# Where one gate product stands, and in which order the first pair's loads, stores and inner sums are issued

## Chip, core and metric

The kernel runs on one core of a Trainium2 chip, in one launch. The metric is device time in microseconds (us), from start to end of the program. The core has engines that run side by side, each with its own queue, strictly in order: TensorE (PE in the profile, PEld for its weight loads), VectorE (DVE), ScalarE (ACT), GpSimd (POOL) and SyncE (SP, which issues most DMA transfers). They wait for each other through semaphores. Matrix products land in PSUM banks, everything else lies in SBUF.

## What is computed

Inputs are x (32 x 128 x 512, float32), a condition vector per batch row, a mask, and the weights of two layers. Here B = 32, S = 128, D = 512, the inner width of the second layer is 1024, everything is float32.

```python
m = mask[:, :, None]
emb = silu(t) @ ada_w + ada_b
shift, scale, gate_msa = split(emb, 3, axis=1)
norm = layernorm(x) * (1.0 + scale[:, None]) + shift[:, None]
norm = where(m, norm, 0.0)
fwd = gelu(norm @ ssm_w1 + ssm_b1) @ ssm_w2 + ssm_b2
bwd = flip(gelu(flip(norm) @ bwd_w1 + bwd_b1) @ bwd_w2 + bwd_b2)
x = x + gate_msa[:, None] * where(m, fwd + bwd, 0.0)

ff_ada = silu(t) @ ffada_w + ffada_b
shift_mlp, scale_mlp, gate_mlp = split(ff_ada, 3, axis=1)
ff_norm = layernorm(x) * (1.0 + scale_mlp[:, None]) + shift_mlp[:, None]
h = gelu_tanh(ff_norm @ ff_w1 + ff_b1)
out = x + gate_mlp[:, None] * (h @ ff_w2 + ff_b2)
```

The two flips cancel, because the network works on each token alone. The first layer touches masked tokens only.

## The kernel before

**First layer ("opening").** The masked tokens get numbers, "slots". Four tiles of 128 slots are gathered from x (L254, issued by POOL). In the opening and up to the end of the pairs the program order is the order on every engine: `tc.manual_schedule` (L385) takes PE, DVE, ACT, POOL and SP as they are written.

The condition's product with ada_w has three column blocks: shift, scale and gate. `ada_a` holds the weights; its shift and scale columns come in four loads (L128), its gate columns in a fifth (L132, through L146). `modulation_matmuls` (L279) forms `pm_ss`, the first two blocks; `modulation_rows` (L289) adds the bias on DVE and writes `mod1`. `slot_part` (L299, `part_s`) spreads rows of `mod1` over the slots with a one-hot matrix; there are four of these, scale and shift for slot tiles 0 and 1. Then comes the gate block in another way: four products `pm_g` (L541), one for each quarter of the depth, side by side in strips of 32 partitions; ACT copies them to `gate_parts` (L544); a product with `strips` (L594, `pm_gate`) adds the four. DVE normalises the slot tiles (L182, L183: `xn_s`), PE transposes them (L190, `ptr_s`), ACT copies the transposes (L191), and `hidden_of_tile` (L574, `ph_s`) starts the hidden layer.

`count_more` (L641) takes eight small DVE steps on a product `pt` (L645). Its results serve a loop after the pairs for masked tokens beyond the slots.

**Second layer ("pairs").** All tokens pass in four pairs; a pair is two sides of four batch rows, 1024 tokens. Both products of the layer are formed by a fast scheme of seven instead of eight block products (P1 to P7), with sums before and after. The first product uses it twice, one in the other: seven outer blocks, here called streams, in the order 1, 2, 5, 6, 3, 7, 4, each of seven inner products. One inner product is four matmuls on PE (L988). "P3 of 2" below is inner product P3 of stream 2.

- `weight_sums(j)` (L634) forms four outer sums of the first weight on DVE. `store_weight_sums` (L638, L639) writes them to `t_rows` in DRAM by SP; their homes are borrowed: number 1 in the spare x tiles, 2 in t_2, 4 in `tw_4`. `load_weights(j)` (L934, tile `tw`) reads one back.
- `TokenBlocks.one` (L857) forms the outer sums of the tokens on DVE; its fourth writes into the memory of `tw_4`.
- `token_sums(j, n)` forms inner sums of the tokens on DVE, for j = 1 (L917, `sx`), 2 (L921, `xn_sy`), 3 (L924) and 4 (L927), each in four parts n. Both operands lie in SBUF.
- ACT copies P5 of each stream to `p5` (L1002) and other products on (L1046), or applies the GELU (L950). DVE adds after P6 (L1013), P7 (L1018) and P4 (L1023), and `seed` (L1032) fills the bank of the next product. POOL adds `with_p5` (L1039), `after` (L1068) and late sums (L1072), again with both operands in SBUF.
- A stream's P3 and P7 wait for L1013 of the same stream, P2 for `seed`, P4 for L1018. L1013 of streams 6 and 3 waits for POOL's sums.
- `window(new, old)` interleaves P5, P1, P2, P6 of the new stream with P3, P7, P4 of the old one and runs `fills`, steps put behind a place (window, position) by `put`.
- `take_first_half` (L747): eight gathers by POOL, which overwrite the masked tokens of the next pair's x with rows from the first layer (`x1_rows`). They stand in POOL's queue between `with_p5` of stream 2 and that of stream 6.
- `load_side` (L351) loads x of a coming side; `fw2_of.combine` (L342) and L1314 form differences of the second weight `fw2`, loaded at L705.

The part of the first pair that stands before its first window is written out by hand (L1291 to L1314); the first layer's last tile is stored just before it (`with_x`, L1274).

Of the kernel before, what the change touches and what calls it, by code (L numbers as in the profile page):

```python
# [9 lines left out]
F32 = mybir.dt.float32  # L10
# [4 lines left out]
ALU = mybir.AluOpType  # L15
# [7 lines left out]
def kernel(  # L23
# [49 lines left out]
    nc = tc.nc  # L73
    B, S, D = x.shape
    P = 128
# [3 lines left out]
    KC = D // P  # L79
# [113 lines left out]
    def hidden(xT, n, w, bcol, func, name, pool, parts=range(HC), after=None):  # L193

        h = []
        for f in parts:
            ph = ps_h.tile([P, 512], F32, tag="h", name=f"ph_{name}_{f}")
            for k in range(KC):
                nc.tensor.matmul(  # L199
                    ph[:, :n], w[:, k, ts(f, P)], xT[:, k, :], start=(k == 0), stop=(k == KC - 1)  # L200
                )
            t = pool.tile([P, n], F32, tag="h", name=f"h_{name}_{f}", bufs=HC)
            nc.scalar.activation(t, ph[:, :n], func, bias=biasT[:, bcol + f : bcol + f + 1])
            h.append(t)
            for g in (after or {}).get(f, ()):
                g()
        return h
# [79 lines left out]
    def modulation_rows(pm, mod, modb, lo, hi):  # L287
        rows = slice(lo * B, hi * B)
        nc.vector.tensor_tensor(mod[rows], pm[rows], modb[rows], ALU.add)  # L289
# [14 lines left out]
    def slot_part(at, j, pool, tag):  # L304
        return of_slots(pick, at, mod1, j, pool, tag, f"part{j}_s{at}")
# [228 lines left out]
    token_i = find_slots(1, (ps_h, "h"))  # L534
    modulation_matmuls(pm, ada_a, 0, 2, range(KC - 1, KC))
    modulation_rows(pm, mod1, modb_a, 0, 2)
    rows = [(slot_part(c, 1, ps_o, "o"), slot_part(c, 0, *((ps_o, "o"), (ps_h, "h"))[c])) for c in range(2)]
    gate_parts = tp.tile([P, D], F32, tag="t", name="gate_parts")
    pm = ps_t.tile([P, 512], F32, tag="tr", name="pm_g")
    for k in range(KC):  # L540
        nc.tensor.matmul(  # L541
            pm[ts(k, B), :], sT[:, k, :], ada_a[:, k, ts(2, D)], start=True, stop=True
        )
    nc.scalar.copy(gate_parts, pm)  # L544
    xT_s = ssm.tile([P, KC, NH], F32, tag="xT", name="xT_s0", bufs=2)
    xT_t = ssm.tile([P, KC, NH], F32, tag="xT", name="xT_s1", bufs=2)
    xn = group_of_tiles("s")
# [3 lines left out]
        modulated(xc[0], *rows[0], "s0", xn[:, 0], (mv[:, 0, 0:1], rstd)),  # L551
        modulated(xc[1], *rows[1], "s1", xn[:, 1]),
    ]
    fw1 = fwp.tile([P, KC, FF], F32, name="fw1")
    fw2 = fwp.tile([P, HC, D], F32, name="fw2")
    t_1 = fwp.tile([P, 3, KC // 2, FF // 2], F32, name="t_1")
# [33 lines left out]
    hidden_of_tile(0, 0)  # L590
    hidden_of_tile(1, 0)
    transposed_slots(xn_s[1], xT_s[:, :, ts(1, P)], "s1")
    pm = ps_o.tile([P, 512], F32, tag="o", name="pm_gate")
    nc.tensor.matmul(pm[ts(2, B), :], strips, gate_parts, start=True, stop=True)  # L594
    modulation_rows(pm, mod1, modb_a, 2, 3)
    hidden_of_tile(2, 0)


# [37 lines left out]
    def store_weight_sums(*which, queue=nc.sync):  # L636
        for j in which:
            queue.dma_start(t_rows[j - 1, :, 4:], t_sum[j][1][:, :3])  # L638
            queue.dma_start(t_rows[j - 1, :, :4], t_sum[j][0])  # L639

    def count_more():  # L641

        pt = ps_t.tile([P, 512], F32, tag="tr", name="pt")
        for j in range(2):
            nc.tensor.matmul(pt[:, j : j + 1], every[:, j], count, start=True, stop=True)  # L645
# [12 lines left out]
        nc.vector.tensor_copy(more_i, more_f)  # L658
        nc.vector.tensor_scalar(more_i, more_i, 7, None, ALU.logical_shift_right)
        col_l = const.tile([P, 1], F32, name="col_l")  # L660
        nc.vector.tensor_scalar(col_l, slot_col[:, 0:1], start_at, None, ALU.add)
        return total, start_at, more_i, col_l


    total, start_at, more_i, col_l = count_more()
    for n, t in enumerate(raw):
        own_statistics(t, 2, f"x_{n}")
    h1 = []
# [19 lines left out]
    nc.vector.tensor_tensor(b2, b2, b2b, ALU.add)  # L688
    b2_row = dram.tile([1, D], F32, name="b2_row")
    with_gated_bias(0, gs[0])  # L690
    h1 += hidden(xT_s, NH, w1, 0, AF.Gelu, "s0", ssm, range(3, HC - 1))
    gate_and_next_tile(1)
    Weights(fw1, KC // 2, FF // 2, t_1).combine(0, 1, 2, 3)
# [8 lines left out]
    finish_slots(1, h1, gs[1])  # L702
    nc.sync.dma_start(b2_row, b2[0:1, :])
    broadcast_rows(fb2, ff_b2, nc.sync)
    nc.sync.dma_start(fw2, ff_w2.rearrange("(k p) f -> p k f", p=P))  # L705

    for c in range(2):
        transposed_slots(xn_late[c], xT_t[:, :, ts(c, P)], f"s{2 + c}")
# [535 lines left out]
    def turn_rows(b):  # L1244
# [6 lines left out]
    after[7] += [  # L1251
        normalised_of_side_1,
        lambda: weight_sums(4),
        lambda: store_weight_sums(1, 2, 4),
        lambda: x_of.update({1: [load_side(1, 0, spare), None]}),
        turn(0),
    ]
# [30 lines left out]
    first_half.close()  # L1288
    hp = straight.enter_context(tc.tile_pool(name="hp", bufs=1))
    gp = straight.enter_context(tc.tile_pool(name="gp", bufs=1))  # L1290
    x_of[1][1] = load_side(1, 1)  # L1291
    now = FirstProduct(0, of_x[0].cut(), of_w)
    for j in (1, 2):
        now.load_weights(j)
    for n in range(4):
        now.token_sums(1, n)
    now.apart(1)
    now.do(1, "P1")
    now.seed(1)
# [1 line left out]
    now.do(1, "P5", "P2", "P6")  # L1301
    now.do(2, "P5")
    now.seed(2)
    now.do(1, "P7")
    now.with_p5(2, "22")
    for n in range(4):
        now.token_sums(2, n)
    now.do(1, "P3")
    now.with_p5(2, "12")
    take_first_half(1, x_of[1])  # L1310
    now.do(2, "P2", "P6")
    now.do(1, "P4")
    fw2_of.combine(0, 1)
    nc.vector.tensor_tensor(fb2_step, fb2[:, D // 2 :], fb2[:, : D // 2], ALU.subtract)  # L1314
    for p in range(NP):
        more_pairs = p + 1 < NP
        xs = x_of[p]
# [2 lines left out]
        def put(w, n, f, *args):  # L1320
            fills.setdefault(w, {}).setdefault(n, []).append(lambda: f(*args))

        if p:
            for n, at in enumerate(((1, 3), (1, 4), (1, 6))):
                put(*at, now.token_sums, 2, 1 + n)
        for n, at in enumerate(((1, 6), (2, 1), (2, 3), (2, 3)) if p else ((2, 3), (2, 3), (2, 4), (2, 4))):
            put(*at, now.token_sums, 3, n)
        for n, at in enumerate(((2, 4), (2, 4), (2, 6), (2, 6)) if p else ((2, 6), (2, 6), (3, 1), (3, 1))):
            put(*at, now.token_sums, 4, n)
        put(3, 6, now.load_weights, 3)  # L1330
        put(4, 6, now.load_weights, 4)
        second = SecondProduct(p, now.h, xs)
        put(6, 0, now.late_gelu, "11")
        put(6, 1, second.seed, 0)
        put(6, 3, second.first_block, 0, 0, 2)
# [227 lines left out]
```

## Time and profile before

| what | us |
|---|---|
| timed runs, median of 4 | 465.69 (464.8 to 466.64) |
| profiled execution, its time | 463.53 |
| its span, first to last instruction | 461.8 |
| PE busy, 0 to 10 | 6.05 |
| PE busy, 10 to 20 | 8.10 |
| PE busy, 90 to 100 | 7.94 |
| PE busy, 100 to 110 | 9.39 |
| PE busy, 110 to 120 | 9.34 |
| PE busy, 130 to 380 | 249.98 |

Times in the trace count from the start of the span. A group line gives start, busy time, engine, source line, operation, output <- inputs, count; in brackets stands the idle time of the engine before it and what ended it. A line of waits says who waited for whom, us in total, how often, and the longest.

On all other engines there is slack: DVE is busy for 334.9 us, POOL for 156.7, ACT for 176.5. In 100 to 110 DVE is busy for 9.96 us and in 110 to 120 POOL for 9.51.

### The profile page before, as it was taken

Reading aid. Unit: us, or ns where it says so; the run is one execution under the profiler, and the core shown is the slowest. Engines: PE = TensorE matmul, PEld = TensorE weight load, DVE = VectorE, ACT = ScalarE, POOL = GpSimd, SP = SyncE. Lnnn points to the kernel's source line nnn. Section 1 sums busy time; section 2 is a strip of 40 time slices with the busy share of each in tenths; the row PEclk is TensorE's granted clock in tenths of the full one; section 3 lists DMA queues with packets and bytes.
Section 4 is the critical chain, followed back from the end, with each engine's and each line's share of the span. In section 5 each row is a group of like instructions: output and inputs, shape, how many; then the busy total and the mean of one; then the engine's idle time right before and its main releaser. Section 6 shows DMA issues by size and latency. Waiting matters only on the chain.

```text
span 461.8 us, 5878 instructions
## 1 busy us (share of the span) xinstructions
PE 447.1 (97%) x2026; PEld 366.1 (79%) x2026; DVE 334.9 (73%) x549; ACT 176.5 (38%) x381; POOL 156.7 (34%) x147
## 2 busy tenths in 40 slices
PE   6899999979999999999999999999999999999995
PEld 2484476668888888888888888888888887888884
DVE  5698768799679749896786498957973995434645
ACT  3130032634355371344455514454355154552000
POOL 4220170058971000489700005987000026660000
PEclk9999999999999999999999999999999999999999
DMA  8999587972307743923077249320772442222022
GB/s 280 388 392 384 180 219 135 316 276 36 149 0 217 104 91 126 338 81 117 3 227 114 71 159 321 97 83 11 229 105 66 148 149 80 81 90 94 0 87 99
DMA packets 82755, 70.95 MB, mean 154 GB/s; under 512 B 63136, under 2 KB 63664, under 8 KB 81698
## 3 DMA queue, kind: packets, MB, share of 16 engines
q1 hardware_dynamic: 67874, 58.47, 41.1%
q0 software_dynamic: 4064, 10.54, 6.5%
q10 hardware_dynamic: 10784, 1.52, 2.2%
q8 instruction: 17, 0.28, 0.3%
q14 instruction: 16, 0.13, 0.1%
HBM read 56.84 MB, written 13.70 MB: 153 GB/s over the span
## 4 chain that ended last, share of the span: by engine, by line
PE 91%; DMA 3%; DVE 3%; POOL 1%; issue 1%; ACT 0%; DVEq 0%
PE a_o L1175 23%; PE a_m L988 18%; PE e_o L1175 18%; PE e_m L988 14%; PE po_s L216 6%; PE ph_s L199 5%; DMA tw<-t_rows 1%; DMA xc<-in_x_dram,token_i_s 1%; PE ph_s L574 1%; PE part_s L299 1%; PE pm_f L279 1%; PE last L1175 1%; POOL x L747 1%; DMA mask_u<-in_mask_BxS_bk_dram 0%; PE ptr_s L190 0%
## 5 line engine op out<-in xcount | busy, mean ns | idle before, releaser
L1039 POOL TENSOR_TENSOR ha<-p_m,ha 128x512 f32<-128x512 f32 x20 | 26.2, 1308 | 151.4 <-ACT ha L1046 142.0
L1175 PE MATMUL e_o<-fw,ha 128*128 128x256 f32 x256 | 57.9, 379 | 0.0
L810 ACT ACTIVATE xT<-xT,modT 128x128 f32<-128x128 f32 x112 | 44.2, 479 | 32.1 <-DMA xT<-xn 29.7
L1175 PE MATMUL a_o<-t,hb 128*128 128x256 f32 x240 | 54.1, 379 | 0.0
L1175 PEld LDWEIGHTS e_o<-fw,ha 128*128 128x128 f32 x256 | 48.6, 190 | 6.6
L1175 PEld LDWEIGHTS a_o<-t,hb 128*128 128x128 f32 x240 | 45.6, 190 | 6.2
L950 ACT ACTIVATE hb<-hb,biasT 128x256 f32<-128x256 f32 x64 | 29.0, 500 | 27.6 <-POOL hb L1072 19.3
L1039 POOL TENSOR_TENSOR hb<-p_m,hb 128x512 f32<-128x512 f32 x20 | 29.0, 1452 | 27.2 <-DVE hb L1018 26.8
L1002 ACT COPY p_m<-e_m 128x512 f32<-128x512 f32 x27 | 15.8, 586 | 49.9 <-PE e_m L988 46.0
L747 POOL DMA_INDIRECT x<-x_rows,slot_i x24 | 29.0, 1210 | 6.3 <-issue 5.4
L1046 ACT COPY ha<-e_m 128x512 f32<-128x512 f32 x32 | 18.6, 580 | 28.0 <-PE e_m L988 26.6
L1175 PE MATMUL a_o<-fw,ha 128*128 128x256 f32 x128 | 28.9, 379 | 0.0
L1175 PE MATMUL e_o<-fw,s 128*128 128x256 f32 x128 | 28.9, 379 | 0.0
L1175 PE MATMUL a_o<-t,s 128*128 128x256 f32 x128 | 28.9, 379 | 0.0
L216 PE MATMUL po_s<-w,h_s 128*128 128x512 f32 x64 | 28.3, 592 | 0.0
L1013 DVE TENSOR_TENSOR e_m<-a_m,ha 128x512 f32<-128x512 f32 x20 | 13.9, 697 | 18.1 <-POOL ha L1039 6.7
L1175 PEld LDWEIGHTS e_o<-fw,s 128*128 128x128 f32 x128 | 24.3, 190 | 3.3
L1175 PEld LDWEIGHTS a_o<-t,s 128*128 128x128 f32 x128 | 24.3, 190 | 3.3
L1175 PEld LDWEIGHTS a_o<-fw,ha 128*128 128x128 f32 x128 | 24.3, 190 | 3.3
L950 ACT ACTIVATE ha<-e_m,biasT 128x256 f32<-128x256 f32 x48 | 20.1, 469 | 14.3 <-PE e_m L988 10.3
L988 PE MATMUL a_m<-xT,tw 128*128 128x256 f32 x96 | 24.6, 379 | 0.0
L988 PE MATMUL e_m<-s,fw 128*128 128x256 f32 x92 | 23.6, 379 | 0.0
(226 smaller groups left out, 885.8 us busy)
## 6 DMA issues: line engine op xcount, KB each, us to landing
tw<-t_rows SPq DMA_DIRECT2D x16, 896.0 KB
x<-in_x_dram SPq DMA_DIRECT2D x16, 512.0 KB
gate<-gate_rows POOLq DMA_DIRECT2D x8, 1024.0 KB
out_dram<-x SPq DMA_DIRECT2D x15, 512.0 KB
xT<-xn SPq DMA_DIRECT2D x92, 64.0 KB
fw<-in_L_cond_ff_w_dram SPq DMA_DIRECT2D x2, 2048.0 KB
ada_f<-in_L_cond_ffada_w_dram SPq DMA_DIRECT2D x4, 768.0 KB
ada_a<-in_L_cond_ada_w_dram SPq DMA_DIRECT2D x4, 512.0 KB
```

Source lines behind the costliest of these rows:

```text
L199: nc.tensor.matmul(ph[:, :n], w[:, k, ts(f, P)], xT[:, k, :], start=(k == 0), stop=(k == KC - 1))
L216: nc.tensor.matmul(po, h[f][:, ts(i, P)], w[:, f, :], start=(f == 0), stop=(f == HC - 1))
L279: nc.tensor.matmul(pm[ts(j, B), :], sT[:, k, :], ada[:, k, ts(j, D)], start=(k == 0), stop=(k == KC - 1),)
L747: nc.gpsimd.indirect_dma_start(out=raw[i // 2][:, i % 2] if p == 0 else xs[i // G][i % G // 2][:, i % 2], out_offset=None, in_=x1_rows if ...
L810: nc.scalar.activation(out, src, AF.Identity, bias=shift, scale=scale)
L950: nc.scalar.activation(dst[:, n], src[:, n], AF.Gelu_apprx_tanh, bias=biasT[:, f : f + 1])
L988: nc.tensor.matmul(bank[:, ts(n, QT)], self.w_block(j, product)[:, ts(n, P)], self.x_block(j, product), start=(product in ("P1", "P5") and ...
L1002: nc.scalar.copy(p5, e)
L1013: nc.vector.tensor_tensor(e, a, p5, add)
L1039: nc.gpsimd.tensor_tensor(self.place(RESULT[j], c), self.p5[j], other, ALU.add)
L1046: nc.scalar.copy(self.place(RESULT[j], c), src)
L1175: nc.tensor.matmul(part, src[:, k, ts(i, P)], w[product][:, k, :], start=(last and k == 0), stop=True, skip_group_check=True,)
```

## The change

In the opening, the gate products and the copy to `gate_parts` are issued ahead of the four `part_s`, and the sum `pm_gate` right behind them, in a bank of another PSUM pool. The gate products are then formed once more, into a tile `pm_keep_clock` that nobody reads. The bias of the gate follows behind the two normalised slot tiles. The DVE steps of `count_more` come later; its two small products stay where they are. The load of `fw2` moves from the first layer to behind the second load of weight sums in the first pair. The weight sums are stored in the order 4, 1, 2. In the hand-written part of the first pair, the first load of weight sums comes ahead of the x load; the inner sums are issued between the products; P3 of stream 1 comes ahead of its P7, and so `with_p5` for "12" ahead of that for "22"; the inner sums for j = 3 and 4 come earlier. The differences of `fw2` move to windows 4 and 5. The later pairs keep their order.

```diff
@@ opening
+    def gate_strips(name):
+        pm = ps_t.tile([P, 512], F32, tag="tr", name=name)
+        for k in range(KC):
+            nc.tensor.matmul(
+                pm[ts(k, B), :], sT[:, k, :], ada_a[:, k, ts(2, D)], start=True, stop=True
+            )
+        return pm
+
+    gate_parts = tp.tile([P, D], F32, tag="t", name="gate_parts")
+    nc.scalar.copy(gate_parts, gate_strips("pm_g"))
     rows = [(slot_part(c, 1, ps_o, "o"), slot_part(c, 0, *((ps_o, "o"), (ps_h, "h"))[c])) for c in range(2)]
-    gate_parts = tp.tile([P, D], F32, tag="t", name="gate_parts")
-    pm = ps_t.tile([P, 512], F32, tag="tr", name="pm_g")
-    for k in range(KC):
-        nc.tensor.matmul(
-            pm[ts(k, B), :], sT[:, k, :], ada_a[:, k, ts(2, D)], start=True, stop=True
-        )
-    nc.scalar.copy(gate_parts, pm)
+    pm = ps_h.tile([P, 512], F32, tag="h", name="pm_gate")
+    nc.tensor.matmul(pm[ts(2, B), :], strips, gate_parts, start=True, stop=True)
+    gate_strips("pm_keep_clock")
...
         modulated(xc[1], *rows[1], "s1", xn[:, 1]),
     ]
+    modulation_rows(pm, mod1, modb_a, 2, 3)
...
     transposed_slots(xn_s[1], xT_s[:, :, ts(1, P)], "s1")
-    pm = ps_o.tile([P, 512], F32, tag="o", name="pm_gate")
-    nc.tensor.matmul(pm[ts(2, B), :], strips, gate_parts, start=True, stop=True)
-    modulation_rows(pm, mod1, modb_a, 2, 3)
...
-    total, start_at, more_i, col_l = count_more()
...
     with_gated_bias(0, gs[0])
+    total, start_at, more_i, col_l = count_more()
...
-    nc.sync.dma_start(fw2, ff_w2.rearrange("(k p) f -> p k f", p=P))
...
-        lambda: store_weight_sums(1, 2, 4),
+        lambda: store_weight_sums(4, 1, 2),
@@ first pair
+    now = FirstProduct(0, of_x[0].cut(), of_w)
+    now.load_weights(1)
     x_of[1][1] = load_side(1, 1)
-    now = FirstProduct(0, of_x[0].cut(), of_w)
-    for j in (1, 2):
-        now.load_weights(j)
-    for n in range(4):
-        now.token_sums(1, n)
+    now.load_weights(2)
+    nc.sync.dma_start(fw2, ff_w2.rearrange("(k p) f -> p k f", p=P))
     now.apart(1)
     now.do(1, "P1")
     now.seed(1)
...
     now.do(1, "P5", "P2", "P6")
     now.do(2, "P5")
     now.seed(2)
+    for n in range(2):
+        now.token_sums(1, n)
+    now.do(1, "P3")
+    now.with_p5(2, "12")
     now.do(1, "P7")
     now.with_p5(2, "22")
-    for n in range(4):
+    take_first_half(1, x_of[1])
+    for n in range(2, 4):
+        now.token_sums(1, n)
+    for n in range(2):
         now.token_sums(2, n)
-    now.do(1, "P3")
-    now.with_p5(2, "12")
-    take_first_half(1, x_of[1])
     now.do(2, "P2", "P6")
+    for n in range(2, 4):
+        now.token_sums(2, n)
     now.do(1, "P4")
-    fw2_of.combine(0, 1)
-    nc.vector.tensor_tensor(fb2_step, fb2[:, D // 2 :], fb2[:, : D // 2], ALU.subtract)
+    now.token_sums(3, 0)
...
-        for n, at in enumerate(((1, 6), (2, 1), (2, 3), (2, 3)) if p else ((2, 3), (2, 3), (2, 4), (2, 4))):
-            put(*at, now.token_sums, 3, n)
-        for n, at in enumerate(((2, 4), (2, 4), (2, 6), (2, 6)) if p else ((2, 6), (2, 6), (3, 1), (3, 1))):
+            put(1, 6, now.token_sums, 3, 0)
+        for n, at in enumerate(((2, 1), (2, 3), (2, 3))):
+            put(*at, now.token_sums, 3, 1 + n)
+        for n, at in enumerate(((2, 4), (2, 4), (2, 6), (2, 6))):
             put(*at, now.token_sums, 4, n)
...
+        if p == 0:
+            put(4, 1, fw2_of.combine, 0)
+            put(4, 3, fw2_of.combine, 1)
+            put(
+                5, 1, nc.vector.tensor_tensor,
+                fb2_step, fb2[:, D // 2 :], fb2[:, : D // 2], ALU.subtract,
+            )
```

More of the change, by code (lines that the diff above doesn't have):

```diff
@@ L639, in store_weight_sums @@
             queue.dma_start(t_rows[j - 1, :, :4], t_sum[j][0])
+    pt = ps_t.tile([P, 512], F32, tag="tr", name="pt")
+    for j in range(2):
+        nc.tensor.matmul(pt[:, j : j + 1], every[:, j], count, start=True, stop=True)
     def count_more():
-        pt = ps_t.tile([P, 512], F32, tag="tr", name="pt")
-        for j in range(2):
-            nc.tensor.matmul(pt[:, j : j + 1], every[:, j], count, start=True, stop=True)
         totals = const.tile([P, 2], F32, name="totals")
```

## The prediction

> **What bounds the kernel now.** I read the page first, then busy time by stretch, then what TensorE (PE) waited for.
>
> ```profile
> span 461.8 us, 5878 instructions
> PE 447.1 (97%) x2026; PEld 366.1 (79%) x2026; DVE 334.9 (73%) x549; ACT 176.5 (38%) x381; POOL 156.7 (34%) x147
> ...
> 20.00:90.00 70.00, 70.00 (x289) 43.48 (x288) 54.52 (x108) 19.91 (x42) 13.96 (x16) 1.00 0.85 280
> ...
> PE a_m_alone L988 <- DVE e_m L1013: 1.6, 1, 1.6
> PE e_m L988 <- DVE e_m L1032: 1.1, 2, 0.8
> PE e_m L988 <- DMA tw<-t_rows: 1.1, 1, 1.1
> PE part_s L299 <- DVE mod L289: 0.8, 1, 0.8
> PE ptr_s L190 <- DVE xn_s L183: 0.6, 1, 0.6
> ```
>
> PE is the bound: 447.1 of 461.8 us. From 20 to 90 it works 70.00 of 70 us (second column after the stretch), so a delay before 20 arrives at 90 undiminished. Idle time lies in two places that the change touches: the opening (0.8 + 0.6) and the first pair (1.6, 1.1 and two of 0.3). Nothing in the change removes matmuls, so about 4 us is the most it could gain. The timelines of the two places (start, us, engine, line):
>
> ```profile
> 6.32 4.57 PE L279 MATMUL pm_ss<-ada_a,sT 128*32 128x512 f32 x12
> 11.45 1.05 PE L279 MATMUL pm_ss<-ada_a,sT 128*32 128x512 f32 x4
> 13.29 1.99 PE L299 MATMUL part_s<-mod,pick 32*128 32x512 f32 x8 [0.79 <-DVE mod L289]
> 14.07 0.37 SPq L132 DMA_DIRECT2D w<-in_L_cond_bwd_w_dram  x1
> 15.20 1.06 PE L541 MATMUL pm_g<-ada_a,sT 128*32 128x512 f32 x8
> 16.90 0.66 PE L190 MATMUL ptr_s<-ident,xn_s 128*128 128x128 f32 x4 [0.63 <-DVE xn_s L183]
> 20.67 1.05 PE L594 MATMUL pm_gate<-gate_parts,strips 128*32 128x512 f32 x2
> ...
> 88.86 1.23 DVE L857 TENSOR_TENSOR s<-xT,s 128x1024 f32<-128x1024 f32 x1 [2.20 <-DMA t_rows<-tw]
> 94.94 1.13 PE L988 MATMUL a_m_alone<-xT,t 128*128 128x256 f32 x4 [1.58 <-DVE e_m L1013]
> 97.31 3.43 DVE L921 TENSOR_TENSOR xn_sy<-sx,xT 128x512 f32<-128x512 f32 x2
> 98.49 1.71 POOL L1039 TENSOR_TENSOR ha<-p_m,ha 128x512 f32<-128x512 f32 x1
> 100.61 1.10 PE L988 MATMUL e_m<-sx,tw 128*128 128x256 f32 x4 [1.09 <-DMA tw<-t_rows]
> 101.99 1.69 POOL L747 DMA_INDIRECT x<-x_rows,slot_i  x1 [0.30 <-issue]
> 103.99 1.00 POOL L747 DMA_INDIRECT x<-x_rows,slot_i  x1 [0.30 <-issue]
> ...
> SPq L132 <- DMA ada_a<-in_L_cond_ada_w_dram: 4.6, 2, 3.2
> ```
>
> **Opening.** Before, PE is free at 12.50 (11.45 + 1.05) and waits for the mod rows until 13.29. Now pm_g stands in that pause. But the gate columns it reads are the last load of ada_w. SP shows when they land: its load at 14.07 reuses that load's semaphore (the new program's pm_g waits on the same one), and of SP's waits on ada_a the long one, 3.2 us, ends there. So pm_g starts at 14.05, not 12.50. It holds PE for 0.95 (its 1.06 less the overlap with the next group): part_s at 15.0. From part_s to the next group takes 1.82 (15.20 - 13.29, less 0.1 for refilling after a wait): 16.84. pm_gate 0.97 (20.67 to 21.64): 17.8. The product nobody reads, 0.9 like pm_g: 18.7. Only then ptr_s, 1.8 later than 16.90. VectorE (DVE) is no longer what it waits for: the first two part_s end at 16.05, two 0.75 us steps make xn_s by 17.6. Behind it everything is as before, except that pm_gate (0.97) and a refill are gone from 20.67. Net +0.75. If the columns were there at 12.50, the same sum gives -0.7; these are the ends. I take +0.75, since SP's wait measures the landing.
>
> **The clock.** In the rows, six pm_ss passes from 6.32 took 0.76 us each (4.57/6), the two at 11.45 took 0.53; the pauses of 0.79, 0.63 and 0.48 after that left the clock alone. So I cost the 1.55 us pause at 12.50 at nothing, and the unread product at its 0.9. The Trainium skill (TensorE: Matmul & The Clock Gate, Part 1) has the clock fall only after an idle window of about 3.4 us. By it the unread product buys nothing here either, and the sum stays; it speaks against that edit.
>
> **First pair, up to the first sum.** Groups of four matmuls start 0.864 apart, their result is there 1.03 after the start, and a wait adds 0.1. With +0.75, P6 of stream 1 ends at 93.26 and P5 of stream 2 at 94.12. Store order: DVE's L857 at 88.86 waited 2.20 for the store of tw, the last of six; that store now goes second, 3.8 us earlier on SP (78.85 against 82.69). L857 still needs ScalarE's 16 scalings (80.96 + 6.27 = 87.23), so it gains 1.6. The price: the x loads of the next side overwrite the tiles of what is now the third and fourth store, so they wait for those; the fourth is issued at 80.45 and lands by 86.5 if it takes the 6.1 us of the tw store (82.69 to the 88.8 that DVE waited for), against 83.97 now. That is hidden: their first reader is the gather at 100.36. With the four inner sums no longer ahead, L1013 follows P6 at once, 93.32 to 94.01, and P3 of 1 starts at 94.07 where before P7 of 1 started at 94.94: -0.87 at this point.
>
> **Where that goes.** The sums run after L1032 (waits for the copy of P5, 94.8) from 95.44, just where POOL starts its first sum (95.91: end of P3, 95.20, plus a 0.6 copy). Both read two SBUF operands, and the row at 97.31 shows what happens then: two L921 took 3.43 instead of 2 x 0.68, each held about 1.1 by a POOL sum. So the second inner sum ends at 97.91, L1018 runs 97.83 to 98.52, and P4 of 1, which needs it, starts at 98.58 against 98.50: the 0.87 is gone. The next product, P5 of 5, gains: load_weights(1) is issued ahead of the 1 MB x load as soon as DVE frees SP (po_s done at 88.9, then three steps of 0.7: 91.1, against 92.1), so tw is there before 98 (6.84 us in the chain with the x load ahead of it) and P5 starts at 99.54 against 100.61. POOL's second sum (98.6 to 100.3) holds the fourth inner sum; two sums of j=2 follow; L1013 of 2 runs 101.76 to 102.45; P3 of 2 starts at 102.51 against 102.41. Two waits, 0.95 and 1.24, stand for the 1.6 and 1.1 removed.
>
> **Gathers and fw2.** POOL's eight gathers start at 100.26 (before 100.36), behind its two sums. Before they took 12.6 us, 1.58 each: 1.30 from start to start where no two-operand DVE sum ran (103.99), up to 2.0 where one did. The fw2 differences (1.21 + 1.23 + 0.45) leave this stretch, so I take 1.40, between 1.30 and 1.58. They end by 111.46; four POOL sums and L1032 later P2 of 3 starts at 116.43 against 117.49. Both waits of 0.33 are gone. Now the fw2 differences come: the first waits for a POOL sum, runs 116.32 to 117.53, holds the next POOL sum; the second runs 118.64 to 119.86 and holds the POOL sum that L1013 of 3 needs (before 120.41, now 121.11). P3 of 3 starts at 121.86 against 121.91, and after two waits of 0.2 and 0.3 P4 of 3 at 126.01 against 125.36: **+0.65**. From there POOL has pauses (2.7 us before 131.06) and PE none until 380, so it stays. fw2 itself, 2 MB issued behind 2.8 MB from 91.5, is there by 108.5 at the 290 GB/s of that stretch; first use 116. Spacing 1.30 would make the sum +0.24, 1.50 +1.45, 1.58 +2.1.
>
> A rule differs from these rows. The Trainium skill (SBUF — State Buffer, Who interferes with whom) infers that a two-input DVE sum does not stall descriptor generation on GpSimd; the gathers at 101.99 and 103.99, 1.69 and 1.00, say it does. By the rule spacing is 1.30 and the sum +0.24; by the rows +0.65.
>
> **Moved at no cost:** the eight count_more steps (0.15 each) leave DVE's queue at 22.97 for a place before the second late tile; PE is never short there. Their PSUM tile stays open longer, its successor comes only at 51.8. Pairs two to four are untouched.
>
> **Rivals.** (1) The sums do not meet on the port: then P4 of 1 starts at 97.6, P3 of 2 at 100.2, 2.2 earlier than before, gathers 1.4 earlier: -2.2, 463.5. For it: one slipped operation changes who holds whom. Against: L921 is held in all four pairs of the trace. (2) POOL as the bound, on the slower side: its gathers keep 1.58, end at 112.9, and P3 of 6, then P2 of 3, wait, and the fw2 differences come on top: +2.1, 467.8. It decides once the last gather ends later than about 111.9. For it: DVE now has twelve two-operand sums in that stretch; against: they total less time than before. (3) The 1.55 us pause drops the clock: the 3.4 us from 6.32 to 9.7 ran at half rate, so +1.7 on top of +0.65: 468.0. (4) The product stands in no pause because its data is late; that is in the forecast.
>
> **Numbers.** The profiled execution took 463.53 (span 461.8), below the four timed runs (464.8 to 466.64, median 465.69). I put +0.65 on the median: **466.3**. Chances: forecast, no measurable change, 0.57; rival 1 0.18; rival 2 0.20; rival 3 0.05. A measurement of this kernel tells 0.3%, 1.4 us, from no change; so faster 0.18, same 0.57, slower 0.25. Range 463.5 to 467.9: it reaches to rivals 1 and 2.
>
> **What would show it.** pm_g's start (14.05, or near 12.5); ptr_s near 18.7; a wait at P4 of 1 and at P3 of 2 of about 1 us; an inner sum of stream 1 (L922 there, L917 now) of 1.7 us beside a POOL sum; last gather's end near 111.5; waits at P3 of 3. I am wrong if inner sums of stream 1 take 0.68 throughout, or if the gate columns land before 13.

## The result, and the profile after

After: 464.78 us, median of 44 runs (463.38 to 471.85). Before, in the same comparison: 464.89, median of 70 (463.22 to 467.46). The ratio is 1.0009, 95% interval 0.9997 to 1.002: no measurable change, +0.4 us with -0.1 to +0.9 around it. The ratio goes by the mean times and leaves out the one slow run of after (471.85 us); the medians alone differ by -0.1. The prediction had +0.65, and 466.3 as the time, because it counted from a median of before of 465.69 over four runs; over the 70 runs that median is 464.89.

The profiled execution of after took 466.24 (span 464.5), 2.7 more than that of before. So its trace shows more loss than the median has; the experiments below separate what belongs to the kernel from what belongs to that execution. From the page:

```profile
span 464.5 us, 5898 instructions
...
PE 449.0 (97%) x2034; PEld 367.1 (79%) x2034; DVE 338.7 (73%) x549; ACT 176.5 (38%) x381; POOL 156.3 (34%) x147
```

The waits of TensorE (total us, times, longest), without a wait of 3.2 at the very start and three of 0.3 to 0.5, which both kernels have:

```profile
...
PE a_m L993 <- DVE hb L1023: 2.2, 1, 2.2
PE pm_g L541 <- DMA ada_a<-in_L_cond_ada_w_dram: 1.7, 1, 1.7
PE e_m L993 <- DVE e_m L1018: 1.0, 1, 1.0
PE e_m L993 <- DVE e_m L1037: 0.8, 1, 0.8
PE a_m_alone L993 <- DVE hb L1023: 0.6, 1, 0.6
...
```

PE's busy time rose by 1.9 though no matmul but the unread product (0.9) was added: something ran slower. The waits of before (1.6, 1.1 and two of 0.3 in the first pair; 0.8 and 0.6 in the opening) are gone; 2.2, 1.0 and 0.6 in the first pair and 1.7 in the opening stand in their place (the 0.8 is in the last pair, in both kernels). The opening (start, us, engine, line):

```profile
11.77 1.05 PE L279 MATMUL pm_ss<-ada_a,sT 128*32 128x512 f32 x4
14.47 1.07 PE L541 MATMUL pm_g<-ada_a,sT 128*32 128x512 f32 x8 [1.65 <-DMA ada_a<-in_L_cond_ada_w_dram]
15.47 1.99 PE L299 MATMUL part_s<-mod,pick 32*128 32x512 f32 x8
19.22 0.66 PE L190 MATMUL ptr_s<-ident,xn_s 128*128 128x128 f32 x4
22.89 1.06 PE L582 MATMUL ph_s<-xT_s,w 128*128 128x128 f32 x8
```

The gate product waits for its columns, as forecast; the third hidden block starts at 22.89 where before had 21.64. And the stretch of the first pair in which the time goes, PE first, then VectorE and POOL beside it:

```profile
115.60 1.03 PE L993 MATMUL e_m<-xT,fw 128*128 128x256 f32 x4
116.46 1.03 PE L993 MATMUL a_m<-s,t 128*128 128x256 f32 x4
119.74 1.99 PE L993 MATMUL a_m<-xn_sy,tw 128*128 128x256 f32 x4 [2.25 <-DVE hb L1023]
121.52 1.89 PE L993 MATMUL e_m<-s,tw 128*128 128x256 f32 x4
123.23 1.05 PE L993 MATMUL a_m<-xT,tw 128*128 128x256 f32 x4
124.12 1.03 PE L993 MATMUL e_m<-s,fw 128*128 128x256 f32 x4
...
114.97 4.11 DVE L342 TENSOR_TENSOR t<-fw 128x1024 f32<-128x1024 f32 x1
119.00 0.68 DVE L1023 TENSOR_TENSOR hb<-a_m,hb 128x512 f32<-128x512 f32 x1
...
114.30 1.26 POOL L1044 TENSOR_TENSOR ha<-p_m,ha 128x512 f32<-128x512 f32 x1
115.52 1.25 POOL L1044 TENSOR_TENSOR hb<-p_m,hb 128x512 f32<-128x512 f32 x1
116.74 1.25 POOL L1073 TENSOR_TENSOR ha<-ha 128x512 f32<-128x512 f32 x1
119.83 2.11 POOL L1073 TENSOR_TENSOR hb<-hb 128x512 f32<-128x512 f32 x1 [1.83 <-DVE hb L1023]
```

The first fw2 difference, 1.2 us of work, lies on VectorE for 4.11 us, until the third of three POOL sums in a row is done. Behind it in VectorE's queue stands the sum after P7 of stream 6 (L1023); P4 of stream 6 needs that, and PE pauses for 2.25 us. Then two groups take 1.78 and 1.71 from start to start in place of 0.864: PE runs at half rate.

Counted from the start of P1 of stream 1 (the first column under each kernel is measured in its profile, the prediction's from its text, with P1 at before's 88.02 plus its 0.75):

| start of | before | predicted | after | fw2 differences late (below) |
|---|---|---|---|---|
| P1 of stream 1, us | 88.02 | 88.77 | 88.23 | 87.14 |
| P4 of 1 | +10.48 | +9.81 | +9.63 | +9.64 |
| P3 of 2 | +14.39 | +13.74 | +13.45 | +13.46 |
| P2 of 3 | +29.47 | +27.66 | +27.37 | +27.38 |
| P4 of 3 | +37.34 | +37.24 | +39.34 | +35.14 |
| second product | +44.25 | | +46.25 | +42.05 |

### The profile page after: what moved, and what is told of

Its sections match the earlier page's. It is cut to its first block, busy times and chain, and to the rows that moved or that the text cites. A ratio compares the mean times of both kernels' runs of the same rounds, so it can differ in the third digit from the quotient of the medians.

```text
span 464.5 us, 5898 instructions
## 1 busy us (share of the span) xinstructions
PE 449.0 (97%) x2034; PEld 367.1 (79%) x2034; DVE 338.7 (73%) x549; ACT 176.5 (38%) x381; POOL 156.3 (34%) x147
## 4 chain that ended last, share of the span: by engine, by line
PE 62%; DVE 10%; SPq 7%; POOL 5%; ACT 5%; issue 5%; DMA 5%; POOLq 0%; ACTq 0%; DVEq 0%
PE a_m L993 14%; PE a_o L1180 11%; PE e_m L993 11%; PE e_o L1180 9%; SPq L832 6%; PE po_s L216 6%; PE ph_s L199 5%; ACT xT L815 3%; DMA ada_a<-in_L_cond_ada_w_dram 2%; DMA xT<-xn 2%; POOL x L752 2%; DVE t_o L1154 1%; PE part_s L299 1%; PE ph_s L582 1%; POOL hb L1077 1%
## 5 line engine op out<-in xcount | busy, mean ns | idle before, releaser
L752 POOL DMA_INDIRECT x<-x_rows,slot_i x24 | 27.6, 1151 | 6.3 <-issue 5.4
```

The lines of the kernel that those rows point to most:

```text
L752: nc.gpsimd.indirect_dma_start(out=raw[i // 2][:, i % 2] if p == 0 else xs[i // G][i % G // 2][:, i % 2], out_offset=None, in_=x1_rows if ...
```

## The experiments

Each ratio is to runs of before that were made beside the experiment's. "After's fw2 place" means windows 4 (behind P1 and behind P7), as in the diff shown above.

**The kernel before, again.**

> The kernel before, unchanged, for the granted clock of its timed runs (of the kernel after, 44 runs show mean clocks from 0.986 to 1.0; of the kernel before only one is known, 0.999). Theory: its longest pause on TensorE in the first pair, 1.58 us, drops the clock in few executions or none; nearly all runs at 0.997 or above, median 464.9, and the longer runs (up to 467.5) are the ones with a lower mean clock. Rival: the clock falls about as often as after (25 of 44 runs below 0.998), so it has nothing to do with the 2.25 us pause.

Ratio 0.9996 (0.9981 to 1.0011), median 464.91. The rival is nearer: of its 12 runs five have a mean clock of 0.994 or 0.995, and these took no longer (464.09 to 465.15) than those at 1.0 (464.05 to 466.8). A part of the lower clock can fall at the end, where PE has nothing left: the clock record of every profile here closes with a stretch at half rate of 1.6 to 4.8 us, which begins between 2.8 us before the last instruction and 0.5 us after it. That accounts for a mean clock down to 0.997; where the rest of a mean of 0.994 lies no profile shows. But as these runs are no longer than the others, a mean clock of 0.994 by itself says nothing about this change. In this execution P1 started at 88.41.

**The fw2 differences put late**, and the same kernel again.

```diff
-            put(4, 1, fw2_of.combine, 0)
-            put(4, 3, fw2_of.combine, 1)
+            put(6, 1, fw2_of.combine, 0)
+            put(6, 3, fw2_of.combine, 1)
```

> After, with the two fw2 differences behind P1 and behind P7 of the window of streams 7 and 4, where POOL paused for 2.7 us. Theory: the first of them was held by three POOL sums in a row (4.11 us) and this alone made TensorE wait 2.25 us at P4 of 6; moved, that wait is gone, each difference takes 1.2 to 1.9 us, the granted clock does not fall in the first pair, the first block of the second product starts at 130.9 (134.48 after, 132.27 before), and the median is 462.6, with hardly any run above 465. Rival: POOL's chain of sums was the limit anyway and the wait comes back at P3 or P4 of stream 3 with over 1.5 us: median 464 or more.

> The kernel with the fw2 differences put late, a second time, as the base for the two that follow. Theory: median 461.5 again, 0.7% below before; no pause in the first pair above 1 us, so no half-rate stretch, and no run above 464. Rival: the first six runs were lucky in when the loads land: median 462.5 or more.

Ratio 0.9931 (0.9912 to 0.9951), median 461.48, and again 0.9938 (0.9925 to 0.9951), median 461.97. No run of the eleven is above 462.5. The medians expected were 462.6 and 461.5. It is faster than before by about 0.7%, where after is not. VectorE and POOL of the first of the two:

```profile
125.75 1.21 DVE L342 TENSOR_TENSOR t<-fw 128x1024 f32<-128x1024 f32 x1
127.49 1.21 DVE L342 TENSOR_TENSOR fw<-fw 128x1024 f32<-128x1024 f32 x1
...
123.18 1.27 POOL L1077 TENSOR_TENSOR ha<-ha 128x512 f32<-128x512 f32 x1 [0.95 <-ACT ha L1051]
127.98 1.84 POOL L1077 TENSOR_TENSOR ha<-ha 128x512 f32<-128x512 f32 x1 [2.52 <-ACT ha L1051]
```

Both differences take 1.21 in POOL's pause; all that is left is one POOL sum of 1.84 in place of 1.27. P4 of 6 starts 0.86 behind the group ahead of it, without a wait. The table's last column shows that up to P2 of 3 nothing differs from after (+27.38 against +27.37), and that all of the difference, 4.2 us at P4 of 3, comes from this one place. The rival, a wait that returns at stream 3, is out.

**The first difference in two halves**, at after's fw2 place.

```diff
-                nc.vector.tensor_tensor(out, x, y, ALU.subtract)
+                parts = [slice(None)]
+                if j in halved:
+                    n = out.shape[1] // 2
+                    parts = [slice(0, n), slice(n, 2 * n)]
+                for part in parts:
+                    nc.vector.tensor_tensor(out[:, part], x[:, part], y[:, part], ALU.subtract)
...
-            put(4, 1, fw2_of.combine, 0)
+            put(4, 1, lambda: fw2_of.combine(0, halved=(0,)))
```

> After, with the first fw2 difference as two instructions of half the width (128x512, the width of the inner sums) at the same place. Theory A: VectorE gets the port only when POOL has no next sum ready, which it has until it lacks the P7 sum of stream 6 that stands behind the differences on VectorE: the first half takes about 3.5 us, the second 0.6, and TensorE's wait at P4 of 6 stays at 2.2 to 2.4. Theory B, the prediction's reading of the inner sums: each two-operand instruction waits for the one POOL sum that runs: the halves take 1.8 each or less, and the wait at P4 of 6 is under 1.2.

One profiled execution, no timed runs:

```profile
118.21 1.13 PE L998 MATMUL a_m<-xn_sy,tw 128*128 128x256 f32 x4 [2.31 <-DVE hb L1028]
...
113.38 4.18 DVE L347 TENSOR_TENSOR t<-fw 128x512 f32<-128x512 f32 x2
...
122.65 1.54 DVE L1335 TENSOR_TENSOR fb_step<-fb 128x256 f32<-128x256 f32 x1
```

The two halves took 4.18 together, the wait at P4 of 6 was 2.31. These are theory A's numbers, and theory B is out: the width isn't the reason, and one difference can wait for several POOL sums. Here VectorE got in when POOL had no sum left, because POOL lacked the very sum that stood behind the difference on VectorE. Theory A's "only when POOL has no next sum ready" is more than the traces bear, though. In the last line, 9 us later in the same execution, VectorE waited for one POOL sum (122.64 to 123.91) and ran ahead of the next, which POOL started at 123.86 without a pause and which took 1.47. In before, inner sums got in between two POOL sums in the same way (the prediction's rows at 97.31 and 98.49). What decides between the two is not shown.

**Both differences ahead of L1023.**

```diff
-                put(4, 3, fw2_of.combine, 1)
+                put(4, 1, fw2_of.combine, 1)
```

> After, with the second fw2 difference put directly behind the first, so that both stand ahead of the P7 sum of stream 6. Theory: the first is held as before (4.1 us), the second runs freely (1.2), TensorE's wait at P4 of 6 is 3.4 us in place of 2.25. A fixed grid of 3.413 us windows sets the clock: half rate follows a window in which TensorE was busy for less than about 0.4 (0.34 after, which dropped; 0.43 without the opening's edit, which did not). 3.4 us of pause leave such a window in some three of four executions, so the median is 1.1 us above after's for the wait and another 1 to 1.7 for the clock: about 467.3. Rival: only a window without any work drops it, so hardly ever: 465.9 and a mean clock above 0.998.

Wait 3.52 at P4 of 6 (3.4 expected; first 4.11, second 1.22). Ratio 1.0084 (1.0051 to 1.0117), median 468.73, more than the 467.3 expected. The one run at a mean clock of 1.0 took 464.11, the five at 0.989 or less 469.9 to 472.0; that is more than one stretch of half rate costs, and where further ones lie no profile shows. The profiled execution is the one at 1.0, and it shows why it escaped. The clock record of each profile gives the edges of its half-rate stretches; they lie a multiple of 3.413 us apart, so the grid of that execution can be laid over its trace. Busy time in the windows of that grid follows (window, its length, the busy us of PE and the other engines; the granted clock is the third number from the end, ahead of DMA share and GB/s). After:

```profile
116.44:119.86 3.42, 1.17 (x6) 0.69 (x5) 3.42 (x3) 0.84 (x2) 1.59 (x3) 1.00 0.00 0
119.86:123.27 3.41, 3.41 (x9) 2.70 (x10) 3.38 (x6) 0.00 (x0) 2.42 (x2) 0.50 0.17 21
123.27:126.68 3.41, 3.41 (x17) 3.02 (x16) 2.33 (x5) 1.42 (x3) 3.38 (x3) 1.00 0.61 248
```

Both differences ahead of L1023:

```profile
114.40:117.82 3.42, 1.68 (x8) 1.14 (x6) 3.38 (x2) 0.84 (x2) 2.19 (x2) 1.00 0.05 17
117.82:121.23 3.41, 1.63 (x8) 1.46 (x9) 3.38 (x6) 0.00 (x0) 1.27 (x1) 1.00 0.00 0
121.23:124.64 3.41, 3.41 (x17) 3.02 (x16) 3.21 (x6) 1.43 (x3) 2.99 (x3) 1.00 0.76 269
```

After with the opening of before (an experiment below), whose pause is 2.25 too:

```profile
116.92:120.33 3.41, 1.46 (x7) 1.31 (x8) 3.41 (x4) 0.00 (x0) 1.58 (x2) 1.00 0.02 5
120.33:123.74 3.41, 3.41 (x16) 2.63 (x15) 3.34 (x8) 1.42 (x3) 2.42 (x3) 1.00 0.77 265
```

Before, again, with its 2.14 ahead of P7 of 1:

```profile
92.09:95.50 3.41, 1.67 (x8) 1.13 (x6) 3.38 (x7) 1.66 (x3) 0.00 (x0) 1.00 0.48 122
95.50:98.91 3.41, 3.02 (x14) 2.68 (x15) 2.78 (x5) 0.71 (x2) 1.02 (x1) 1.00 1.07 418
```

In after the whole pause of 2.25 fell into one window: PE was busy for 1.17 of 3.42, and the next window ran at 0.50. In this kernel a longer pause, 3.52, was cut in two by the edge, 1.68 and 1.63 were left, and the clock stayed. With 1.46 and 1.67 busy it stayed too. So the same kernel may lose its clock or not, by where the grid lies in that execution: in these windows the bound lies between 1.17 and 1.46 busy of 3.41. The ends of the executions narrow it: the last window with work in the profile of the opening alone (454.95 to 458.37) held 1.41 of PE and was followed by half rate, and the one in the repeat of fw2 late (454.07 to 457.48) held 1.69 and was not. That PE's busy time is what counts fits all these windows; nothing else was varied to test it.

**fw2 undone**: its load and its differences where before has them, the new order of inner sums kept.

```diff
@@ first layer
+    nc.sync.dma_start(fw2, ff_w2.rearrange("(k p) f -> p k f", p=P))
@@ first pair
-    nc.sync.dma_start(fw2, ff_w2.rearrange("(k p) f -> p k f", p=P))
...
     now.do(1, "P4")
     now.token_sums(3, 0)
+    fw2_of.combine(0, 1)
+    nc.vector.tensor_tensor(fb2_step, fb2[:, D // 2 :], fb2[:, : D // 2], ALU.subtract)
...
-        if p == 0:
-            put(4, 1, fw2_of.combine, 0)
-            put(4, 3, fw2_of.combine, 1)
...
```

> After, with fw2's load and its two differences where before had them (differences behind P4 of stream 1, load ahead of the first product). Counted from P1 of stream 1. Theory: no difference runs beside back-to-back POOL sums, so the wait at P4 of 6 is gone; but the differences meet the gathers, whose spacing is 1.5 to 1.6 instead of 1.36, so P2 of 3 comes at +28.5 (+27.4 after, +29.5 before) and the second product at +43.3 (+46.3 after with its clock drop, +44.3 before, +42.05 with the differences put late): median about 463. Rival: the gathers don't mind the differences: second product at +42.1, as with the differences put late.

Ratio 1.0101 (1.0064 to 1.0139), median 469.53: both theory and rival fell. Two of TensorE's waits there:

```profile
106.63 1.13 PE L994 MATMUL a_m<-xT,t 128*128 128x256 f32 x4 [1.78 <-DVE hb L1024]
114.36 1.31 PE L994 MATMUL e_m<-xn_sy,tw 128*128 128x256 f32 x4 [2.99 <-DVE e_m L1038]
```

The differences ran freely (1.21 and 1.23 from 102.53) and the gathers, from the first start to the last end, took 1.39 each (99.14 to 110.29; 1.36 in after, 1.58 in before), but in VectorE's full queue they made the sum after P7 of stream 2 late: a wait of 1.78. Later one inner sum was held for 3.52 us by the last gather and the two POOL sums behind it, and PE waited 2.99. In the window of that pause, on the 3.413 us grid, PE was busy for 0.82, and the next ran at half rate. So with the inner sums' new order the differences cost more in before's place than in after's: the second product starts at P1 + 49.19, where after has +46.25, and +42.05 with the differences put late.

**The opening alone**: before, with the gate product, the unread product and the count steps as after has them.

> Before, with the opening of after alone (gate product ahead of the slot parts, unread product, count steps later). Theory: third hidden block near 22.9 against 21.64, but P1 of stream 1 at 88.2 against 88.02, and the median 0.2 above that of before. Rival, as the prediction had it: the delay arrives undiminished: P1 at 89.2, median 1.1 above before. If instead the opening gains by itself: P1 below 87.8.

Ratio 0.9985 (0.9963 to 1.0008), median 463.4: no measurable change. P1 at 87.45, so neither theory nor rival, but the third branch: in this execution the gate columns were there early (SP's load behind them at 12.87, pm_g at 12.95 without a wait), and the third hidden block started at 21.36.

**The old opening**: after, with before's opening; the count steps stay late.

> After, with the gate product, its row product and the mod rows where they stood before, and without the unread product; the later place of the eight count steps is kept. Theory: the opening's delay (1.15 us at 24) was swallowed at 34 to 36, where TensorE waited for VectorE inside a group that the view of busy time counts as busy, and the count steps' move had brought VectorE forward there by 0.7. So P1 of stream 1 starts at 87.4 (88.23 after, 88.02 before), and the median falls by 0.8 to 464.0. Rival: the pause at 34 takes the gain too: P1 at 88.0, median 464.6. The wait at P4 of 6 stays near 2.2 in both.

P1 at 87.36 as the theory had it, wait at P4 of 6 of 2.25; but median 465.84, where the theory had 464.0 and the rival 464.6; ratio 1.0013 (0.9998 to 1.0029). So the 0.8 did not show in the median, and against the 1.0009 of after the two openings show no difference.

**The count steps alone**: before, with the eight steps behind the gated bias.

> Before, with one edit: the eight count steps behind the gated bias, as after has them. Theory: they held VectorE's chain to the second late tile, for which TensorE waited at 34 to 36 inside a group that counts as busy; that group (six slot-part products) takes 1.1 to 1.4 us in place of 2.2 to 2.5, P1 of stream 1 starts at 87.5 (88.02 and 88.41 before), and the median is 0.8 below that of before. Rival, the prediction's 'moved at no cost': P1 at 88.0 or later, median unchanged.

The theory fell in the profiled execution: P1 at 88.61, and the group at 34 took 2.67. VectorE's chain behind which it waits:

```profile
24.77 0.69 DVE L168 BATCH_NORM_STATS2 st_x<-x 128x6 f32<-128x512 f32 x1 [2.15 <-DMA x<-in_x_dram]
34.84 0.75 DVE L183 SCALAR_TENSOR_TENSOR x<-x,rstd_s,part_s 128x512 f32<-128x512 f32 x1
```

With the count steps out of the way, VectorE waited 2.15 us for the x tiles, until 24.77, later than the 24.30 at which before began the same step behind the count steps. The row of before is

```profile
24.30 0.69 DVE L168 BATCH_NORM_STATS2 st_x<-x 128x6 f32<-128x512 f32 x1
```

Median 464.01, ratio 0.9982 (0.9963 to 1.0001). That is about the 0.8 less that the theory had, but the interval just reaches no change, so the runs neither confirm nor refute it.

The four together, with the other profiles, sorted by SP's load behind the gate columns (it tells how early that execution's loads landed):

| kernel | SP's load, us | opening | count steps | P1 of stream 1 |
|---|---|---|---|---|
| opening alone | 12.87 | new | late | 87.45 |
| both differences ahead | 12.97 | new | late | 86.82 |
| halves | 13.00 | new | late | 86.64 |
| late, no unread product | 13.04 | new | late | 87.33 |
| stores and loads | 13.09 | old | early | 87.98 |
| old opening | 13.21 | old | late | 87.36 |
| fw2 late | 13.50 | new | late | 87.14 |
| fw2 undone | 13.51 | new | late | 87.68 |
| fw2 late, again | 13.97 | new | late | 88.12 |
| before | 14.07 | old | early | 88.02 |
| count steps alone | 14.36 | old | late | 88.61 |
| after | 14.40 | new | late | 88.23 |
| inner sums behind | 14.42 | new | late | 88.06 |
| before, again | 14.43 | old | early | 88.41 |

Where the loads are late, P1 stands at 88.0 to 88.6 with either opening; where they are early and the count steps late, at 86.6 to 87.7, again with either. With the late landing P1 comes about 1 us later; the place of the gate product shows less than the rows scatter. These are 14 single executions of several kernels, and within the early ones P1 doesn't follow the landing further. The one row with early loads and early count steps (87.98) suggests that the count steps are worth 0.3 to 1.3 then; it is one execution.

**Without the unread product**, from the kernel with fw2 late.

```diff
-    gate_strips("pm_keep_clock")
```

> The kernel with the fw2 differences put late, without the product that nobody reads. Theory: where the opening's loads land early (SP's load behind the gate columns at 13.5 or before) TensorE is the limit up to P1 of stream 1 and gains the product's 0.9: third hidden block at 21.1, P1 near 86.3; where they land late (14.0 to 14.4) VectorE's chain behind the x tiles sets P1 and nothing is gained; median 0.4 below the kernel with it, and no half-rate stretch in the opening. Rival: without it the clock falls in the opening, a row of 128x512 products there takes twice 0.12 us a piece and P1 comes at 88 or later.

Median 461.99, no lower than with the product (461.48 and 461.97), ratio 0.9957 (0.993 to 0.9984); the profile has P1 at 87.33, where the theory had 86.3 for early loads, and no half-rate stretch between the opening and the end. The third hidden block did start at 20.93, but a wait at 72 took it back:

```profile
72.11 0.33 PE L820 MATMUL ptr<-ident,xn 128*128 128x128 f32 x1 [0.92 <-DVE xn L774]
```

PE is there before VectorE's normalised tile. In the repeat of fw2 late the same wait is 0.30. So there are two places, 34 and 72, at which a gain of the opening can be lost, and here none arrived. Three of the twelve runs took 466 to 468.9 at a mean clock of 0.984 to 0.988. With the product none of eleven did; so few runs can't settle whether it helps.

**Inner sums behind the sum for P3 of 2**, from the kernel with fw2 late.

```diff
-    for n in range(2):
-        now.token_sums(2, n)
     now.do(2, "P2", "P6")
-    for n in range(2, 4):
+    for n in range(4):
         now.token_sums(2, n)
```

> The kernel with the fw2 differences put late, with the first two inner sums of j=2 behind VectorE's sum for P3 of stream 2 instead of ahead of it. Theory: the wait of 0.96 at P3 of 2 goes (P3 of 2 at P1 + 12.4, 13.46 before), but POOL, with eight gathers and three sums in a row, lets P2 of 3 gain 0.5 at most (P1 + 26.9, 27.4 before, with a wait of 0.3 to 0.5 ahead of it): second product at P1 + 41.5 (42.05), median 0.5 lower. Rival: the moved sums lengthen the gathers' spacing and the gain is lost: P2 of 3 at P1 + 27.4 or later.

The wait of 0.96 went, and the rival was right: the gathers began at 99.53 and the last ended at 111.60, 1.51 each, where the kernel with the sums ahead has 1.36. P2 of 3 came at P1 + 28.08 with a wait of 0.45, the second product at +42.85 (42.05). Ratio 1.0003 (0.997 to 1.0036); of twelve runs five are at 466.4 to 469.1 with a mean clock of 0.991 or less. The rest lie at 461.7 to 463.6 but for one (467.74).

**Stores and loads alone**: before, with store order 4, 1, 2 and the load of the first weight sums ahead of x.

```diff
-        lambda: store_weight_sums(1, 2, 4),
+        lambda: store_weight_sums(4, 1, 2),
...
-    x_of[1][1] = load_side(1, 1)
     now = FirstProduct(0, of_x[0].cut(), of_w)
-    for j in (1, 2):
-        now.load_weights(j)
+    now.load_weights(1)
+    x_of[1][1] = load_side(1, 1)
+    now.load_weights(2)
```

> Before, with two edits of the change: store order 4, 1, 2, and the load of the first weight sums ahead of that of x. Inner sums and fw2 stay as before. Counted from P1 of stream 1. Theory: the last TokenBlocks step no longer waits for a store (2.2 us), the inner sums run earlier, and P7 of 1 starts 0.9 earlier (+6.1 against +6.9 to +7.5), P5 of 5 without its wait for tw (+10.6 against +12.5); POOL's gathers keep their spacing, so 0.9 is what is left at P2 of 3 (+28.6 against +29.5) and at the second product (+43.4 against +44.3): median 0.9 below before. Rival: POOL takes it back: second product at +44.2, median as before.

Ratio 0.996 (0.9945 to 0.9975), median 462.75, all six runs at 461.9 to 464.2. P7 of 1 at P1 + 6.11 with a wait of 0.77, P2 of 3 at +28.67, second product at +43.45, P5 of 5 at +10.82 without a listed wait: the theory's numbers within 0.1, but for P5 of 5 (10.6). The gain in the median, 1.9, is larger than the 0.9 that this place shows against the first profile of before. Against the second one, which has its second product at +44.82, the place shows 1.4; the rest isn't explained.

## Why the prediction was right, point by point

- **The gate product waits for its columns** (forecast 14.05): 14.47 in after, since the columns landed 0.33 later than in the execution I read it from. The order behind came as worked out: part_s at 15.47 (15.0), ptr_s at 19.22 (18.7), third block 1.25 later than before (forecast 0.75; part_s alone was 0.47 late). The error is that I took one execution's landing for the kernel's: over 14 profiles it lies between 12.87 and 14.43, in two of them ahead of the 13 that I had named as a sign of being wrong.
- **"A delay before 20 arrives at 90 undiminished" failed.** 1.25 at 22.9 was 0.21 at 88. I read it from PE's 70.00 of 70 us busy; but the profile models the ends of matmuls, and small pauses between pipelined groups are covered by that. The waits of the weight loads, which I did not read, show one (before, window 30 to 40):

```profile
PEld ph_s L199 <- ACT gs L309: 0.8, 1, 0.8
PEld part_s L299 <- DVE x L183: 0.6, 1, 0.6
```

The timeline of PE at that place, before:

```profile
33.90 2.26 PE L299 MATMUL part_s<-mod,pick 32*128 32x512 f32 x6
```

And after:

```profile
35.05 1.14 PE L299 MATMUL part_s<-mod,pick 32*128 32x512 f32 x6
```

The same six products take 2.26 and 1.14. Before, PE waited here for VectorE for 1.1 us (the 0.6 in the view of the weight loads is a part of it; the 0.8 stands in after too), and the opening's delay went into that: the next group starts at 36.10 before and 36.12 after. The 0.2 of P1 come back only at 72.55, where PE waits for VectorE once more.

- **"Moved at no cost" for the count steps** was wrong in its reason ("PE is never short there"): PE is short at 34. In before and in the count steps alone, VectorE's chain to that place starts with the later of the count steps and the landing of the x tiles (24.30 and 24.77). So the steps' place should matter only where the loads are early; that rests on these two profiles and on the one row of the table.
- **The clock in the opening and the unread product**: no profile shows a half-rate stretch there, after a pause of 0 to 1.72 ahead of pm_g (the clock records begin between 9.4 and 12.0). What remains open is below.
- **The first pair up to P2 of 3** was right: -1.81 forecast, -2.10 measured, both from P1. The store order let L862 (L857 before) start at 86.79 with no wait for a store, a second and a fourth inner sum were held (1.77 and 1.49 at 95.44 and 98.33), two waits stand for the two removed (0.58 and 0.97; forecast 0.95 and 1.24), and the gathers started at 99.69 and took 1.36 each (forecast 100.26 and 1.40, counted the same way, first start to last end). Rival 1 (no meeting on the port) and rival 2 (gathers at 1.58) are out for this kernel; the experiment with the inner sums behind shows 1.51 when some of the same sums come later.
- **The fw2 differences are the term that was mis-sized.** From P2 of 3 to P4 of 3 I had +1.71; the profile of after has +4.10, that with the old opening, where the clock stayed, +2.89. The step that failed: "the first waits for a POOL sum, runs 116.32 to 117.53". It waited for three, the rest of one and two whole ones. My row was the inner sums at 97.31 of before, where VectorE got in between two POOL sums; here it got in only when POOL had run out. Why the one and not the other isn't shown.
- **Rival 3's mechanism occurs, at another place**: not the pause at 12.50 but the 2.25 at P4 of 6 halves the clock. In after's profile that costs 1.69 (groups of 1.78 and 1.71 for 0.97 and 0.86, and 0.03), and waits of 0.16 and 0.20 that the old-opening profile shows behind it vanish in it. So the clock lengthened that execution by 1.1 (second product at +46.25, +45.14 with the old opening). With the late landing it may make up most of the 1.5 that separates that execution from the median; only one execution of after was profiled.

With the terms as measured: the opening +0.2, the first pair -2.1, fw2 +2.9 without the loss of the clock: +1.0. Against the second profile of before, whose loads landed as late as those of after (14.43 and 14.40), P1 of after is 0.2 earlier (88.23 and 88.41), not later; with that the sum is +0.6, near the measured +0.4 and the forecast's +0.65. In executions that lose the clock there is more. That the forecast met the time is partly luck, because its parts erred to both sides: the opening was put 0.5 to 0.9 too high, fw2 1.2 too low, the first pair 0.3 too high.

## What to carry to other kernels

A delay can vanish where the busy row of the bound engine says that it can't: read the waits of its weight loads too, before calling a stretch full. A VectorE instruction with two SBUF operands may wait for several such instructions of GpSimd in a row; put it where GpSimd pauses (about 0.7% here, from two changed numbers), and look which instruction of VectorE's queue GpSimd will be waiting for. A landing time read from one execution is one draw: here it spread over 1.6 us.

## What the runs showed of the hardware that was not expected

- VectorE does not always get its turn behind one GpSimd instruction. A 128x1024 difference of 1.21 took 4.11 beside three POOL sums of 1.25 in a row, two halves of it 4.18, a 128x512 inner sum 3.52 beside a gather's end and two sums; POOL's rows there weren't lengthened. Elsewhere in the same traces it waited for one: in before two inner sums of 0.68 took 1.76 and 1.75 (together the 3.43 at 97.31), and the POOL sum between them 1.71. The Trainium skill (SBUF — State Buffer, Who interferes with whom) has a VectorE instruction with two SBUF inputs contend with a GpSimd instruction that reads SBUF; the rows agree, and add that the wait can span more than one GpSimd instruction.
- Half rate after a window that isn't idle: 0.82, 1.17 and, at an execution's end, 1.41 us busy of 3.41 were too little, 1.46 were enough, and within the kernel the stretch lasted one window (3.413). The Trainium skill (TensorE: Matmul & The Clock Gate, Part 1) has a free-running window of that length, with which the edges in these traces agree, and the fall after an idle window; here the window that preceded it held four to six matmuls, and a pause of 2.25 us sufficed where it fell into one window.
- The same loads of the opening land between 12.87 and 14.43, and P1 of stream 1, 75 us later, comes about 1 us later with the late ones: in two profiles of one kernel (fw2 late) 13.50 and 13.97, P1 at 87.14 and 88.12.

Not settled: with the new opening and no pause above 1.4 us in the first pair, 10 of 47 runs have a mean clock of 0.992 or less and take 466 to 469 us (2 of 12, 0 of 11, 3 of 12, 5 of 12 in the four kernels); with the old opening 2 of 116. The pause ahead of pm_g, up to 1.72 us, beside the pauses that follow, is the suspect, but no profile caught such an execution, so it isn't shown. It was also not tried to start the gate product later, behind the slot parts, with the late fw2 differences, nor to move the load of fw2 alone.
